# Block sums of the GRU gates over three PSUM tiles, and the last pair's update summed in the transposition

## Chip, cores and metric

One core of a Trainium2 chip. The metric is device time in microseconds, from the program's start to its end; lower is better.

## The reference

Sixty-four graphs of 256 nodes with 256 features. A layer norm with ReLU, then a message-passing layer with a convolution, ended by a GRU cell, and a residual:

```python
h = jnp.maximum(_layernorm(x, axis=-1), 0.0)
# of h: x_conv (two convolutions along the nodes, 1 and 17 taps, batch norms, ReLU, residual)
# of h: x_nmp = (exp(-dist) * adj) @ relu(h @ w_msg.T + b_msg)
x_in = jnp.concatenate([x_conv, x_nmp], axis=-1)
gi = x_in @ w_ih.T + b_ih
gh = h @ w_hh.T + b_hh
r = jax.nn.sigmoid(gi_r + gh_r)
z = jax.nn.sigmoid(gi_z + gh_z)
nn_ = jnp.tanh(gi_n + r * gh_n)
out = x + (1.0 - z) * nn_ + z * h
```

All of it is float32. The 17-tap convolution is done as products at chosen points (an FFT-like scheme in VectorE, products in TensorE), which the change does not touch.

## The kernel before, in words

**Batches, pairs, layout.** The loop `for b in range(NB)` (L1331) takes eight batches of eight graphs, each as four pairs of graphs. A pair's activations lie transposed: features on partitions in two halves (`dc` 0 and 1), and 512 columns, 256 for each of the two graphs (`g` 0 and 1). First comes the batch's convolution by products, then for each of the four pairs the gates (`gates`, L1188), with the next batch's first convolution, affinity and messages woven in.

**The gates.** A gate is a sum of products of weights with `h`, `xn` (x_nmp) and `xc` (x_conv). Both the weights and the activations are cut into two halves (features in and out, graphs), and a product of 2 x 2 blocks is made of seven block products instead of eight, with sums of blocks (`sums`, L1104, in VectorE) and sums of weights prepared ahead. `factors` (L1121) names the seven, and `part` (L1140) issues one of them: 6 matmuls of 256 columns for the r and z gates (`RZ`), 3 for the candidate (`NH`). In the trace each fp32 matmul stands as two instructions. `seven` (L1162) puts the seven together. It is called twice for each pair, first for r and z, then for the candidate.

**PSUM.** There are two rings: `aux`, four tiles of one bank (512 columns), and `acc`, two tiles of two banks (L580, L581). A ring hands its tiles out in the order in which the code asks. In `seven`, tile A = acc holds the sums of feature half 0 (one bank for each graph), E = acc those of half 1, and p5 = aux holds part 5 for a moment. The order recorded is:

- part 1 into A[:, 0]; ScalarE puts its negative into E[:, 0];
- part 5 into p5; ScalarE copies that to `e` in SBUF;
- part 2 onto A[:, 0]; part 6 onto E[:, 0];
- VectorE: A[:, 1] = E[:, 0] + e;
- part 7 onto E[:, 0]; VectorE: E[:, 1] = -E[:, 0] - e;
- part 3 onto A[:, 1]; half 0 is ready, `opened(0, A)`;
- part 4 onto E[:, 0]; half 1 is ready, `opened(1, E)`.

`opened` is `rz` (L1192; two tanh of 512 columns in ScalarE, to `tr` and to the slot of `tz`, shown as wb in the profile) or `n` (L1197; in ScalarE a bias pass and a copy of 512, then VectorE and a tanh for the candidate, the update h' = n + z (h - n), and copies to `back`, which a transposing transfer turns).

**The last pair** has no work after it that could cover its end. Its candidate pass is written out by hand (L1237 to L1253), in tiles of one bank, and ends in `last` (L1216), once for each feature half and graph: a bias pass in ScalarE, two steps in VectorE, tanh, a subtraction from h, a product with z, and two half-size steps that write `y_last`. `finish` (L1255) then transposes the eight 128 x 128 chunks of `y_last` in TensorE, adds x (`x_last`, shown as hh) and stores.

**What sets the order.** Every instruction goes through a `Recorder` (L250 on). It notes what each one reads and writes, and `plan` (L395) then issues all of them in an order of its own: it keeps a clock for each engine from estimated costs, gives every task a latest time counted back from TensorE's total, and takes for each engine the ready task with the earliest such time. So a small edit can change the order of instructions over the whole program. A PSUM tile counts as a whole in these dependences (`m = 1`, L280), both banks of an acc tile together. `nc.behind` adds a dependence by hand, and `nc.joined` keeps the four affinity products in one piece. Each engine then works in order. Since all go through the recorder, the profile puts nearly all of them at L378; instructions are told apart by their tiles. Slots of SBUF are shown as `wb`, whatever they hold.

Of the kernel before, what the change touches and what calls it, by code (L numbers as in the profile page):

```python
# [15 lines left out]
AF = mybir.ActivationFunctionType  # L16
ALU = mybir.AluOpType
# [477 lines left out]
def kernel(  # L495
# [18 lines left out]
    nc = Recorder(tc.nc)  # L514
    P = 128
    B, N, D = x.shape
    G = 2
# [4 lines left out]
    DC = D // P  # L522
    MC = N // P
    W = G * N
# [4 lines left out]
    L = 16  # L529
    NW = N // L  # L530
# [24 lines left out]
    Ut, Vt = (keep(n, SL) for n in ("U", "V"))  # L555
# [3 lines left out]
    ident = keep("ident", P)  # L559
    make_identity(tc.nc, ident)  # L560
    neg_half = keep("neg_half", G * MC)
# [18 lines left out]
    aux = Ring(psum.tile([P, W], FP, name=f"aux{k}") for k in range(4))  # L580
    acc = Ring(psum.tile([P, 2, W], FP, name=f"acc{k}") for k in range(2))  # L581
# [17 lines left out]
    def row_tile(t, g):  # L599
        return t[:, g * MC:(g + 1) * MC, :].rearrange("p c d -> p (c d)")  # L600
# [5 lines left out]
    def chunk(t, g, c):  # L606
        return t[:, g * N + c * P:g * N + (c + 1) * P]
# [3 lines left out]
    X, ADJ, HT, XNM, STATS = {}, {}, {}, {}, {}  # L611
# [117 lines left out]
    mm, transpose = nc.tensor.matmul, (lambda p, v: nc.tensor.transpose(p, v, ident))  # L729
    p = aux()  # L730
# [430 lines left out]

    def seven(i, unit, opened):  # L1162

        A = acc()
        part(A[:, 0], 1, i, unit, True)
        E = acc()
        nc.scalar.mul(E[:, 0], A[:, 0], -1.0)
        p5 = aux()
        part(p5, 5, i, unit, True)
        e = slots[ROLE["e"]].rearrange("p c d -> p (c d)")  # L1170
        nc.scalar.copy(e, p5)
        part(A[:, 0], 2, i, unit)
        part(E[:, 0], 6, i, unit)
        nc.vector.tensor_add(A[:, 1], E[:, 0], e)
        part(E[:, 0], 7, i, unit)
        nc.vector.scalar_tensor_tensor(E[:, 1], E[:, 0], -1.0, e, op0=ALU.mult, op1=ALU.subtract)
        part(A[:, 1], 3, i, unit)
        opened(0, A)
        part(E[:, 0], 4, i, unit)
        opened(1, E)  # L1180

    def halfs(p, k):
        return p[:, :, k * N:(k + 1) * N]

    def pieces(t):
        return t.rearrange("p (g n) -> p g n", n=N)

    def gates(i, between=None):  # L1188
        tr, gn = tr_tile, gn_tile
        tz = [slots[ROLE[f"tz{dc}"]].rearrange("p c d -> p (c d)") for dc in range(DC)]  # L1190

        def rz(dc, p):  # L1192
            for gate, t in ((0, tr[:, dc]), (1, tz[dc])):
                nc.scalar.activation(pieces(t), halfs(p, gate), AF.Tanh,
                                     bias=b_rz[:, gate * DC + dc:gate * DC + dc + 1], scale=0.5 - dc)

        def n(dc, p):  # L1197
            g = gn[:, dc]
            nc.scalar.activation(pieces(g), halfs(p, 1), AF.Identity,
                                 bias=b_hh[:, 2 * DC + dc:2 * DC + dc + 1], scale=1.0 - 2 * dc)  # L1200
            x = XNM[i][:, dc]
            nc.scalar.copy(pieces(x), halfs(p, 0))
# [12 lines left out]

        def last(dc, g, p):  # L1216
            a = slice(g * N, (g + 1) * N)
            v, d = gn[:, dc, a], tr[:, dc, a]
            nc.scalar.activation(v, p[:, N:], AF.Identity,
                                 bias=b_hh[:, 2 * DC + dc:2 * DC + dc + 1], scale=1.0 - 2 * dc)  # L1220
            nc.vector.scalar_tensor_tensor(v, d, 1.0, v, op0=ALU.add, op1=ALU.mult)
            nc.vector.scalar_tensor_tensor(v, v, 0.5, p[:, :N], op0=ALU.mult, op1=ALU.subtract if dc else ALU.add)
            nc.scalar.activation(v, v, AF.Tanh, bias=b_ih[:, 2 * DC + dc:2 * DC + dc + 1])
            nc.vector.tensor_sub(d, HT[i][:, dc, a], v)
            nc.vector.scalar_tensor_tensor(d, tz[dc][:, a], 1.0, d, op0=ALU.add, op1=ALU.mult)
            for c in range(MC):
                t = chunk(y_last[:, dc], g, c).rearrange("p (b h) -> p h b", b=NW)
                u, w = (q[:, c * P:(c + 1) * P].rearrange("p (h b) -> p h b", b=NW) for q in (d, v))
                nc.vector.scalar_tensor_tensor(t, u, 0.5, w, op0=ALU.mult, op1=ALU.add)

        seven(i, RZ, rz)
        if between:
            between()
        if i + 1 < NP:
            seven(i, NH, n)
            return
        a0, p5, e1, a1, e0 = aux(), aux(), aux(), acc()[:, 1], acc()[:, 0]  # L1237
        e = slots[ROLE["e"]].rearrange("p c d -> p (c d)")
        part(a0, 1, i, NH, True)
        nc.scalar.mul(e0, a0, -1.0)  # L1240
        part(p5, 5, i, NH, True)
        nc.scalar.copy(e, p5)
        part(a0, 2, i, NH)
        last(0, 0, a0)
        part(e0, 6, i, NH)
        nc.vector.tensor_add(a1, e0, e)
        part(e0, 7, i, NH)
        nc.vector.scalar_tensor_tensor(e1, e0, -1.0, e, op0=ALU.mult, op1=ALU.subtract)
        last(1, 1, e1)
        part(a1, 3, i, NH)  # L1250
        last(0, 1, a1)
        part(e0, 4, i, NH)
        last(1, 0, e0)  # L1253

    def finish(i):  # L1255
        if i + 1 < NP:
            t = gn_tile.rearrange("p c n -> p (c n)").bitcast(U16)
            nc.sync.dma_start_transpose(out=t.rearrange("p (k n) -> p k n", n=P), in_=back.bitcast(U16))
            if i % PB < PB - 1:
                deliver(i)  # L1260
            return
        for g in (1, 0):
            p, t = aux(), row_tile(x_last, g)
            for c in range(MC):
                for dc in range(DC):
                    transpose(p[:, c * D + dc * P:c * D + (dc + 1) * P], chunk(y_last[:, dc], g, c))
            nc.vector.tensor_add(t, p, t)
            nc.sync.dma_start(out=blocks(out, G * i + g), in_=t)

    def deliver(i):  # L1270
# [40 lines left out]
    b_rz = keep("b_rz", 2 * DC)  # L1311
# [19 lines left out]
    for b in range(NB):  # L1331
        i = b * PB
# [25 lines left out]
        if b == 0:  # L1358
            nc.emit()
            stage_ctx.close()  # L1360
            late = ctx.enter_context(tc.tile_pool(name="late", bufs=1, reuse_waits="tile"))
            w_x = late.tile([P, 3, len(IN), 3, P], FP, name="w_x")
            xnms = Ring(late.tile([P, DC, W], FP, name=f"xnm{k}") for k in range(2))
            gn_tile, tr_tile = (late.tile([P, DC, W], FP, name=n) for n in ("gn", "tr"))
            back = late.tile([P, DC * W], FP, name="back")
            hh, halves = (late.tile([P, 2 * MC, W], U16, name=n) for n in ("hh", "halves"))
            y_last = Ut[:, :DC * W].rearrange("p (c n) -> p c n", c=DC)
            x_last = hh.bitcast(FP).rearrange("p k d -> p (k d)").rearrange("p (q d) -> p q d", d=D)
        aggregate(i)
        begin(4)  # L1370
# [171 lines left out]
```

## Time and profile before

| | |
|---|---|
| median of 3 runs | 1669.55 us (1669.16 to 1672.69) |
| the profiled execution | 1671.88 us |
| its span, first to last instruction | 1670.1 us |
| TensorE busy, share of the span | 99%, 8984 matmul instructions |
| VectorE | 1456.8 us, 87% |
| ScalarE | 1127.2 us, 67% |
| GpSimd | 236.0 us, 14% |
| waits of TensorE for VectorE's acc | 7.8 us, 18 times |

How to read it: PE is TensorE, PEld its weight loads, DVE is VectorE, ACT is ScalarE, POOL is GpSimd, SP the queue of transfers. A group shows output <- inputs, with the tile's number left out. A number in brackets behind an instruction in the timeline is the idle time of its engine just ahead of it, and what ended it. Matmuls overlap, so the duration of a group of n is n steps and some 0.17 us of its last one's drain: 12 instructions of 256 columns last 2.75 us, and the next group starts 2.59 us after them.

### The profile page before, as it was taken

The numbers are of one execution on the slowest core, as the hardware profiler recorded it, in microseconds if no ns is written. First come the engines' busy times: TensorE is split into PE (matmuls) and PEld (weight loads), VectorE is DVE, ScalarE is ACT, GpSimd is POOL, SyncE is SP. The second block draws the span as 40 slices with busy tenths as digits, with TensorE's granted clock in tenths as the row PEclk, the third lists the DMA queues.
The fourth block names the chain that finished last, engine by engine and source line by source line (L and its number), as shares of the span: only waits on it lengthen the run. The fifth ranks groups of instructions, "written<-read, shape, count | busy, mean of one in ns | idle before, by whom it ended". The sixth has DMA issues, their size and how long they took to land.

```text
span 1670.1 us, 26281 instructions
## 1 busy us (share of the span) xinstructions
PE 1645.7 (99%) x8984; PEld 1413.3 (85%) x8984; DVE 1456.8 (87%) x3401; ACT 1127.2 (67%) x2029; POOL 236.0 (14%) x245
## 2 busy tenths in 40 slices
PE   9999999999999999999999999999999999999997
PEld 6888878978899788988889887897889978898886
DVE  7979989889889898898998988988988989789544
ACT  5546766776767767686756776677676776657554
POOL 4210210022110221103110131002211022000000
PEclk9999999999999999999999999999999999999999
DMA  9882557856468455783478654684647845375022
GB/s 250 301 291 75 135 109 203 264 110 147 108 202 227 105 123 126 237 205 95 114 139 265 151 122 103 176 259 110 146 108 207 222 108 133 83 231 142 16 61 51
DMA packets 314936, 261.37 MB, mean 156 GB/s; under 512 B 192875, under 2 KB 240263, under 8 KB 314802
## 3 DMA queue, kind: packets, MB, share of 16 engines
q1 hardware_dynamic: 297010, 216.71, 48.9%
q0 software_dynamic: 17376, 42.66, 11.3%
q8 instruction: 71, 1.16, 0.3%
q14 instruction: 63, 0.52, 0.1%
q10 hardware_dynamic: 416, 0.32, 0.1%
HBM read 156.60 MB, written 43.78 MB: 120 GB/s over the span
## 4 chain that ended last, share of the span: by engine, by line
PE 70%; DVE 24%; DMA 3%; issue 2%; ACT 1%; SPq 0%; DVEq 0%; ACTq 0%
PE acc L378 49%; PE aux L378 21%; DVE V L378 5%; DVE tr L378 3%; DVE U L378 3%; DVE T L378 3%; DVE wb L378 3%; DVE acc L378 2%; DVE gn L378 2%; DMA wb<-filt 2%; DVE st L378 1%; DVE PT L378 1%; DVE msg L378 1%; PE aux L374 1%; DVE Sv L378 0%
## 5 line engine op out<-in xcount | busy, mean ns | idle before, releaser
L378 PE MATMUL acc<-wb,w_ih 128*128 128x256 f32 x768 | 191.9, 379 | 0.0
L378 PEld LDWEIGHTS acc<-wb,w_ih 128*128 128x128 f32 x768 | 145.9, 190 | 19.8
L378 POOL DMA_DIRECT2D back<-in_x_dram x62 | 56.5, 1051 | 727.7 <-ACT back L378 379.5
L378 POOL TENSOR_TENSOR rstd<-rstd,neg_half 128x4 f32<-128x4 f32 x32 | 85.8, 2682 | 458.5 <-DVE shift L378 272.5
L378 PE MATMUL acc<-wb,w_x 128*128 128x256 f32 x576 | 136.9, 383 | 7.8 <-DVE acc L378 7.8
L378 ACT COPY back<-tr 128x512 uint16<-128x512 uint16 x124 | 128.3, 1078 | 22.5 <-DVE tr L378 22.2
L378 DVE SCALAR_TENSOR_TENSOR V<-T,V 128x128 f32<-128x128 f32 (+2 forms) x448 | 141.1, 379 | 0.0
L378 PE MATMUL aux<-wb,w_x 128*128 128x256 f32 x576 | 138.1, 382 | 0.0
L378 PEld LDWEIGHTS acc<-wb,w_x 128*128 128x128 f32 x576 | 106.9, 190 | 36.3 <-DVE acc L378 17.7
L378 PEld LDWEIGHTS aux<-wb,w_x 128*128 128x128 f32 x576 | 108.7, 191 | 17.3 <-DVE wb L378 2.6
L378 PE MATMUL aux<-w_msg,hT 128*128 128x259 f32 x512 | 121.7, 381 | 0.0
L378 PE MATMUL acc<-V,wb 128*128 128x128 f32 x1024 | 118.5, 275 | 0.8 <-DMA wb<-filt 0.8
L378 PEld LDWEIGHTS acc<-U,wb 128*128 128x128 f32 x1024 | 116.9, 192 | 2.6 <-ACT acc L378 1.7
L378 PE MATMUL acc<-U,wb 128*128 128x128 f32 x1024 | 117.2, 275 | 1.6 <-DMA wb<-filt 1.6
L378 PEld LDWEIGHTS acc<-V,wb 128*128 128x128 f32 x1024 | 116.4, 192 | 1.3 <-DMA wb<-filt 1.2
L378 ACT ACTIVATE gn<-acc,bn_columns 128x512 f32<-128x512 f32 (+1 forms) x64 | 43.5, 680 | 106.6 <-PE acc L378 101.5
L378 PE MATMUL acc<-Yv,w_ih 128*128 128x256 f32 x380 | 108.4, 381 | 2.1 <-ACT Yv L378 2.1
L378 PE MATMUL acc<-wb,w_hh 128*128 128x256 f32 x384 | 109.4, 380 | 0.7 <-ACT acc L378 0.7
L378 PEld LDWEIGHTS aux<-w_msg,hT 128*128 128x128 f32 x512 | 96.5, 190 | 14.3
L378 ACT COPY back<-gn 128x1024 uint16<-128x1024 uint16 x62 | 82.8, 1342 | 36.3 <-DMA gn<-back 36.3
L378 PE MATMUL aux<-hT,w_c 128*128 128x512 f32 x224 | 106.1, 592 | 0.0
L378 PE MATMUL acc<-hT,w_hh 128*128 128x256 f32 x380 | 104.0, 380 | 0.0
(200 smaller groups left out, 3898.3 us busy)
## 6 DMA issues: line engine op xcount, KB each, us to landing
wb<-filt SPq DMA_DIRECT2D x348, 256.0 KB
back<-in_x_dram POOLq DMA_DIRECT2D x62, 256.0 KB, 5.0
out_dram<-back POOLq DMA_DIRECT2D x62, 256.0 KB, 2.9
x<-in_x_dram SPq DMA_DIRECT2D x58, 256.0 KB
halves_d<-halves SPq DMA_DIRECT2D x28, 512.0 KB
adjh<-halves_d SPq DMA_DIRECT2D x112, 128.0 KB
hh<-halves SPq DMA_DIRECT2D x108, 128.0 KB
filt<-Yv POOLq DMA_DIRECT2D x18, 224.0 KB, 4.4
```

The lines of the kernel that those rows point to most:

```text
L374: self.tasks[k].call.append(lambda: method(*args, **kw))
L378: self.tasks.append(Task(engine, [lambda: method(*args, **kw)], cost, size, self.first))
```

## The change

It has two parts.

In `seven`, the sums are held in three tiles: a0 is the first bank of an acc tile (its second bank stays unused), a1 is the aux tile that held part 5 and is written over once part 5 has been copied, and E is an acc tile as before. Part 2 is recorded after part 6 and the add. As half 0 now lies in two tiles, `halfs` gives its eviction in two pieces of 256 columns.

For the last pair, the gate factors are brought into their final form before the candidate pass: tr becomes -r, a copy of tz becomes -z (in the free tile of the xnm ring), tz itself becomes z - 1, each in a ScalarE pass of 512 columns, and `z_last` = -z h is formed in VectorE. `last` then takes one VectorE step with the bias in it, one subtraction, the tanh, and one product with z - 1 into `y_last`; two of the four products are put behind the last subtraction. `finish` no longer transposes: products with the identity of `z_last` (behind the last gate matmul) and of `y_last` are summed in the same PSUM tile, and what comes out is subtracted from x.

```diff
     def seven(i, unit, opened):

-        A = acc()
-        part(A[:, 0], 1, i, unit, True)
+        a0 = acc()[:, 0]
+        part(a0, 1, i, unit, True)
         E = acc()
-        nc.scalar.mul(E[:, 0], A[:, 0], -1.0)
-        p5 = aux()
-        part(p5, 5, i, unit, True)
+        nc.scalar.mul(E[:, 0], a0, -1.0)
+        a1 = aux()
+        part(a1, 5, i, unit, True)
         e = slots[ROLE["e"]].rearrange("p c d -> p (c d)")
-        nc.scalar.copy(e, p5)
-        part(A[:, 0], 2, i, unit)
+        nc.scalar.copy(e, a1)
         part(E[:, 0], 6, i, unit)
-        nc.vector.tensor_add(A[:, 1], E[:, 0], e)
+        nc.vector.tensor_add(a1, E[:, 0], e)
+        part(a0, 2, i, unit)
         part(E[:, 0], 7, i, unit)
         nc.vector.scalar_tensor_tensor(E[:, 1], E[:, 0], -1.0, e, op0=ALU.mult, op1=ALU.subtract)
-        part(A[:, 1], 3, i, unit)
-        opened(0, A)
+        part(a1, 3, i, unit)
+        opened(0, (a0, a1))
         part(E[:, 0], 4, i, unit)
         opened(1, E)

-    def halfs(p, k):
-        return p[:, :, k * N:(k + 1) * N]
-
-    def pieces(t):
-        return t.rearrange("p (g n) -> p g n", n=N)
+    def halfs(t, p, k):
+        if isinstance(p, tuple):
+            return [(t[:, g * N:(g + 1) * N], p[g][:, k * N:(k + 1) * N]) for g in range(G)]
+        return [(t.rearrange("p (g n) -> p g n", n=N), p[:, :, k * N:(k + 1) * N])]
...
         def last(dc, g, p):
             a = slice(g * N, (g + 1) * N)
-            v, d = gn[:, dc, a], tr[:, dc, a]
-            nc.scalar.activation(v, p[:, N:], AF.Identity,
-                                 bias=b_hh[:, 2 * DC + dc:2 * DC + dc + 1], scale=1.0 - 2 * dc)
-            nc.vector.scalar_tensor_tensor(v, d, 1.0, v, op0=ALU.add, op1=ALU.mult)
-            nc.vector.scalar_tensor_tensor(v, v, 0.5, p[:, :N], op0=ALU.mult, op1=ALU.subtract if dc else ALU.add)
+            v = gn[:, dc, a]
+            nc.vector.scalar_tensor_tensor(v, p[:, N:], b_hh[:, 2 * DC + dc:2 * DC + dc + 1], tr[:, dc, a],
+                                           op0=ALU.subtract if dc else ALU.add, op1=ALU.mult)
+            nc.vector.tensor_sub(v, *((v, p[:, :N]) if dc else (p[:, :N], v)))
+            put = nc.last["vector"]
             nc.scalar.activation(v, v, AF.Tanh, bias=b_ih[:, 2 * DC + dc:2 * DC + dc + 1])
-            nc.vector.tensor_sub(d, HT[i][:, dc, a], v)
-            nc.vector.scalar_tensor_tensor(d, tz[dc][:, a], 1.0, d, op0=ALU.add, op1=ALU.mult)
-            for c in range(MC):
-                t = chunk(y_last[:, dc], g, c).rearrange("p (b h) -> p h b", b=NW)
-                u, w = (q[:, c * P:(c + 1) * P].rearrange("p (h b) -> p h b", b=NW) for q in (d, v))
-                nc.vector.scalar_tensor_tensor(t, u, 0.5, w, op0=ALU.mult, op1=ALU.add)
+            rest.append((y_last[:, dc, a], v, tz[dc][:, a]))
+            if (dc, g) == (1, 0):
+                for k, r in enumerate(rest):
+                    nc.behind = put if k in (1, 2) else None
+                    turned(*r)
+                nc.behind = None
+
+        def turned(o, u, v):
+            nc.vector.tensor_mul(o.rearrange("p (q b h) -> p q b h", h=L // 2, b=NW),
+                                 *(t.rearrange("p (q h b) -> p q b h", h=L // 2, b=NW) for t in (u, v)))
...
+        z = xnms.tiles[(xnms.n + 1) % 2]
+        for dc in range(DC):
+            for o, v, f in ((tr[:, dc], tr[:, dc], -0.5), (z[:, dc], tz[dc], -0.5), (tz[dc], tz[dc], 0.5)):
+                nc.scalar.activation(o, v, AF.Identity, bias=neg_half[:, :1], scale=f)
+            turned(z_last[:, dc], z[:, dc], HT[i][:, dc])
...
         part(p5, 5, i, NH, True)
         nc.scalar.copy(e, p5)
+        part(e0, 6, i, NH)
+        nc.vector.tensor_add(a1, e0, e)
         part(a0, 2, i, NH)
         last(0, 0, a0)
-        part(e0, 6, i, NH)
-        nc.vector.tensor_add(a1, e0, e)
         part(e0, 7, i, NH)
...
+        ps = [aux() for _ in range(G)]
+        for k, y in enumerate((z_last, y_last)):
+            nc.behind = None if k else nc.last["tensor"]
+            for g in (1, 0):
+                for c in range(MC):
+                    for dc in range(DC):
+                        o = c * D + dc * P
+                        mm(ps[g][:, o:o + P], chunk(y[:, dc], g, c), ident, start=k + o == 0, stop=k == 1,
+                           skip_group_check=True)
         for g in (1, 0):
-            p, t = aux(), row_tile(x_last, g)
-            for c in range(MC):
-                for dc in range(DC):
-                    transpose(p[:, c * D + dc * P:c * D + (dc + 1) * P], chunk(y_last[:, dc], g, c))
-            nc.vector.tensor_add(t, p, t)
+            p, t = ps[g], row_tile(x_last, g)
+            nc.vector.tensor_sub(t, t, p)
             nc.sync.dma_start(out=blocks(out, G * i + g), in_=t)
```

In `rz` and `n` (not shown) each eviction becomes a loop over the pieces that `halfs` returns.

More of the change, by code (lines that the diff above doesn't have):

```diff
@@ L1162, in seven @@
     def seven(i, unit, opened):
-        A = acc()
-        part(A[:, 0], 1, i, unit, True)
+        a0 = acc()[:, 0]
+        part(a0, 1, i, unit, True)
         E = acc()
-        nc.scalar.mul(E[:, 0], A[:, 0], -1.0)
-        p5 = aux()
-        part(p5, 5, i, unit, True)
+        nc.scalar.mul(E[:, 0], a0, -1.0)
+        a1 = aux()
+        part(a1, 5, i, unit, True)
         e = slots[ROLE["e"]].rearrange("p c d -> p (c d)")
-        nc.scalar.copy(e, p5)
-        part(A[:, 0], 2, i, unit)
+        nc.scalar.copy(e, a1)
         part(E[:, 0], 6, i, unit)
-        nc.vector.tensor_add(A[:, 1], E[:, 0], e)
+        nc.vector.tensor_add(a1, E[:, 0], e)
+        part(a0, 2, i, unit)
         part(E[:, 0], 7, i, unit)
         nc.vector.scalar_tensor_tensor(E[:, 1], E[:, 0], -1.0, e, op0=ALU.mult, op1=ALU.subtract)
-        part(A[:, 1], 3, i, unit)
-        opened(0, A)
+        part(a1, 3, i, unit)
+        opened(0, (a0, a1))
         part(E[:, 0], 4, i, unit)
         opened(1, E)
-    def halfs(p, k):
-        return p[:, :, k * N:(k + 1) * N]
-    def pieces(t):
-        return t.rearrange("p (g n) -> p g n", n=N)
+    def halfs(t, p, k):
+        if isinstance(p, tuple):
+            return [(t[:, g * N:(g + 1) * N], p[g][:, k * N:(k + 1) * N]) for g in range(G)]
+        return [(t.rearrange("p (g n) -> p g n", n=N), p[:, :, k * N:(k + 1) * N])]
     def gates(i, between=None):
-        tr, gn = tr_tile, gn_tile
+        tr, gn, rest = tr_tile, gn_tile, []
         tz = [slots[ROLE[f"tz{dc}"]].rearrange("p c d -> p (c d)") for dc in range(DC)]
@@ L1193, in rz @@
             for gate, t in ((0, tr[:, dc]), (1, tz[dc])):
-                nc.scalar.activation(pieces(t), halfs(p, gate), AF.Tanh,
-                                     bias=b_rz[:, gate * DC + dc:gate * DC + dc + 1], scale=0.5 - dc)
+                for o, v in halfs(t, p, gate):
+                    nc.scalar.activation(o, v, AF.Tanh, bias=b_rz[:, gate * DC + dc:gate * DC + dc + 1],
+                                         scale=0.5 - dc)
         def n(dc, p):
             g = gn[:, dc]
-            nc.scalar.activation(pieces(g), halfs(p, 1), AF.Identity,
-                                 bias=b_hh[:, 2 * DC + dc:2 * DC + dc + 1], scale=1.0 - 2 * dc)
+            for o, v in halfs(g, p, 1):
+                nc.scalar.activation(o, v, AF.Identity, bias=b_hh[:, 2 * DC + dc:2 * DC + dc + 1],
+                                     scale=1.0 - 2 * dc)
             x = XNM[i][:, dc]
-            nc.scalar.copy(pieces(x), halfs(p, 0))
+            for o, v in halfs(x, p, 0):
+                nc.scalar.copy(o, v)
             nc.vector.scalar_tensor_tensor(g, tr[:, dc], 1.0, g, op0=ALU.add, op1=ALU.mult)
@@ L1217, in last @@
             a = slice(g * N, (g + 1) * N)
-            v, d = gn[:, dc, a], tr[:, dc, a]
-            nc.scalar.activation(v, p[:, N:], AF.Identity,
-                                 bias=b_hh[:, 2 * DC + dc:2 * DC + dc + 1], scale=1.0 - 2 * dc)
-            nc.vector.scalar_tensor_tensor(v, d, 1.0, v, op0=ALU.add, op1=ALU.mult)
-            nc.vector.scalar_tensor_tensor(v, v, 0.5, p[:, :N], op0=ALU.mult, op1=ALU.subtract if dc else ALU.add)
-            nc.scalar.activation(v, v, AF.Tanh, bias=b_ih[:, 2 * DC + dc:2 * DC + dc + 1])
-            nc.vector.tensor_sub(d, HT[i][:, dc, a], v)
-            nc.vector.scalar_tensor_tensor(d, tz[dc][:, a], 1.0, d, op0=ALU.add, op1=ALU.mult)
-            for c in range(MC):
-                t = chunk(y_last[:, dc], g, c).rearrange("p (b h) -> p h b", b=NW)
-                u, w = (q[:, c * P:(c + 1) * P].rearrange("p (h b) -> p h b", b=NW) for q in (d, v))
-                nc.vector.scalar_tensor_tensor(t, u, 0.5, w, op0=ALU.mult, op1=ALU.add)
+            v = gn[:, dc, a]
[3 more added lines that the diff above has]
+            put = nc.last["vector"]
+            nc.scalar.activation(v, v, AF.Tanh, bias=b_ih[:, 2 * DC + dc:2 * DC + dc + 1])
+            rest.append((y_last[:, dc, a], v, tz[dc][:, a]))
[7 more added lines that the diff above has]
+                                 *(t.rearrange("p (q h b) -> p q b h", h=L // 2, b=NW) for t in (u, v)))
         seven(i, RZ, rz)
@@ L1367 @@
             y_last = Ut[:, :DC * W].rearrange("p (c n) -> p c n", c=DC)
+            z_last = Ut[:, DC * W:2 * DC * W].rearrange("p (c n) -> p c n", c=DC)
             x_last = hh.bitcast(FP).rearrange("p k d -> p (k d)").rearrange("p (q d) -> p q d", d=D)
```

## The prediction

> **What bounds the kernel now.** I read the page first, then TensorE's waits, then its timeline in a middle batch, and last the timeline and the chain of the end. On the page (engine, busy us, share of the span, instructions), and in the seven 198 us stretches that follow each other from 230 us on (one batch each; of which one row):
>
> ```profile
> PE 1645.7 (99%) x8984; PEld 1413.3 (85%) x8984; DVE 1456.8 (87%) x3401; ACT 1127.2 (67%) x2029; POOL 236.0 (14%) x245
> ...
> 626.00:824.00 198.00, 197.03 (x1082) 169.88 (x1081) 179.78 (x421) 139.88 (x249) 28.17 (x24) 1.00 0.62 158
> ```
>
> TensorE is the bound, and nearly full: a batch has under 1 us in which it does nothing. A change can gain only in TensorE's own work, in its few waits, and at the end. These are its waits (who waited for whom: us in all, times, longest):
>
> ```profile
> PE acc L378 <- DVE acc L378: 7.8, 18, 0.7
> PE aux L378 <- DVE U L378: 3.6, 2, 3.4
> PE acc L378 <- DMA wb<-filt: 2.4, 2, 1.6
> PE acc L378 <- ACT Yv L378: 2.1, 1, 2.1
> PE aux L378 <- POOL e L378: 1.8, 1, 1.8
> ...
> PE acc L378 <- ACT acc L378: 0.7, 1, 0.7
> ```
>
> The first row is the change's main target. A middle batch shows what it is:
>
> ```profile
> 426.42 1.89 PE L378 MATMUL acc<-wb,w_ih 128*128 128x256 f32 x8
> 428.24 0.71 PE L374 MATMUL aux<-zT 9*128 9x256 f32 x8
> 429.39 2.86 PE L378 MATMUL acc<-wb,w_x 128*128 128x256 f32 x12 [0.45 <-DVE acc L378]
> ...
> 445.88 1.46 PE L378 MATMUL aux<-e,msg 128*128 128x256 f32 x6
> 447.18 1.46 PE L378 MATMUL acc<-wb,w_x 128*128 128x256 f32 x6
> ```
>
> At 426.42 part 6 of the r and z gates runs. VectorE's add of E[:, 0] and e into A[:, 1] follows it, and part 7 (acc<-wb,w_x) may not overwrite E before that add has read it. Part 2 is spent already, so the planner has only the four affinity products as cover, and TensorE stands 0.45 us. At 445.88, in the candidate gate, six instructions of 1.30 us stand in the same place and there is no wait: that much cover suffices. The wait comes twice in each of the six middle batches and three times in the first and in the last, 18 in all. And the end:
>
> ```profile
> 1653.55 0.70 PE L378 MATMUL acc<-wb,w_hh 128*128 128x256 f32 x2 [0.67 <-ACT acc L378]
> ...
> 1659.26 1.03 PE L378 MATMUL acc<-wb,w_ih 128*128 128x256 f32 x4
> ...
> 1663.81 0.33 PE L378 MATMUL aux<-ident,U 128*128 128x128 f32 x1 [3.37 <-DVE U L378]
> ...
> 1665.34 1.35 DVE L378 TENSOR_TENSOR hh<-aux,hh 128x512 f32<-128x512 f32 x2
> ```
>
> The last gate matmul ends at about 1660.1. Then VectorE and ScalarE work alone (the chain has the stretch from 1660.5 to 1664.3 in VectorE's gn, tr and U, with 0.2 us of issue); eight transposes, two adds of x and the store follow. From the last add's end, 1666.69, to the span's end are 3.4 us of store.
>
> [...] the 0.45 us come back at 627.5, 825.4 and 1023.3. [...] The kernel's recorder is coarser: it treats an acc tile of two banks as one, so the add into A[:, 1] also waits for part 2 in A[:, 0]; that is why part 2 stands before part 6 and is no cover. [...] Here the stretch 1538.0 to 1541.7, after a wait of 2.1 us, has a granted clock of 0.57. [...] The trace has one instruction for a transpose and two for an fp32 product with 128 columns, 0.114 us apart (acc<-U,wb, 64 in 7.32 us at 1510.5).
>
> **The change part by part.**
>
> *Three tiles.* The second sum moves from A's second bank to the aux tile that held part 5. The add no longer touches part 2's tile, so part 2 goes behind part 6. In the changed program's order this holds for every r/z and candidate pass: parts 1, 5, 6, 2, 7, 3, 4, and the affinity products come after the r/z pass. Part 2 has 12 instructions x 0.216 = 2.59 us in r/z and 6 x 0.216 = 1.30 us in the candidate; the add needs some 0.2 us from TensorE's end, 0.70 us for itself and 0.05 us to release, 0.95 us. Both cover it. Gain: 7.8 us, bounds 5 (a third comes back, as VectorE can be in another instruction of up to 1.2 us when part 6 ends) and 7.8.
>
> *Part 6 now comes directly after part 5.* It needs -A in E. In the candidate E becomes free only when the r/z pass's second eviction is done: 0.2 + 2 x 0.59 (tr, wb) + 0.59 (the negation) + 0.05 = 2.0 us after part 4, against parts 1 and 5, 2 x 1.30 = 2.6 us. Hidden, with 0.6 us to spare. Where exps or `back` copies stand between on ScalarE the order has other work between too: affinity 0.9 us, in some pairs conv1, 1.7 us. Cost 0; without that cover 0.3 us in each of 16 passes, 4.8 us.
>
> *ScalarE.* The first sum's eviction is cut in halves: 64 more instructions in r/z, 62 in the candidate. Two of 256 columns cost 0.38 us each, start to start (the two gn tanhs of 256 columns before 1661.6), against 0.59 for one of 512: 0.17 us x 126 = 21 us at most, against 543 us in which ScalarE idles. Who waits: acc's first bank is evicted before part 3 even runs, so the next pass is freed earlier; the aux half has part 4's 2.59 us as cover against 0.2 + 2 x 0.38. Cost 0.
>
> *aux held longer.* a1 keeps one of four aux tiles from part 5 to its eviction, some 14 us rather than 3.5. Affinity and message take all four and so come after part 3. The order shows other parts in their old places. No row prices what is late then: between 0 and 3 us, I take 1.0. SP's transfers and POOL's change place by a few positions; TensorE waits for a transfer only twice, 2.4 us, before the first gate: 0.
>
> *The end.* Per `last` three VectorE instructions and one ScalarE go in place of six and two. Six ScalarE passes of 512 (0.59) and two products of 512 columns (the permuted e<-e,adj of 256 takes 0.51 from start to start, so 1.0 each) come ahead, under parts 1 to 6. On ScalarE only one of them stands before the negation that releases part 6: 0.2 + 3 x 0.59 + 0.59 = 2.6 us against 2.6 of parts 1 and 5. So the 0.67 us wait goes, and part 4 ends some 0.7 to 0.9 us earlier, at about 1659.3. From there: 0.2, the first VectorE step 0.35, the subtraction 0.41, under the two products that are put behind it 0.9 (the tanh, 0.55, hides there), the last product 0.5: 1661.7. TensorE meanwhile does z times h: 8 x 2 x 0.114 = 1.8 us. The y products follow, 1.8 us, half of them before the last factor is there: to about 1662.9; the last subtraction from x, 0.2 + 0.7: 1663.9, where it was 1666.69. Gain 2.8 us with the 0.67 in it; bounds 1.3 (the permuted products take 0.8 each) and 3.6.
>
> Sum: -7.8 - 2.8 + 1.0 = -9.6 us. The profiled execution took 1671.88 us (span 1670.1 and 1.8 around it): 1662.3. The median shown is 1669.55, 2.3 lower; I set the forecast against it: 1660.0.
>
> **The rivals.**
>
> *B, half comes back as waits for ScalarE.* Part 6 lost part 2 as its cover. At 16 passes x 0.3 us = 4.8 us the time is 1669.55 - 9.6 + 4.8 = 1664.8. For it: ScalarE's queue is in order and has 1.3 us copies in it. Against it: only one wait of TensorE for ScalarE's acc is in the trace, 0.7 us.
>
> *C, the waits only move.* Part 2 is no new work; what it covers it leaves uncovered elsewhere. Then the end alone gains: 1669.55 - 2.8 = 1666.8, inside 0.2%. Against it: at 445.88 other work is the cover today; part 2 takes its place, and that work is set free rather than missing.
>
> *D, slower.* ScalarE's `back` copies wait in line for the transposing transfers (36.3 us in 15 waits, the longest 4.8). In the changed order they stand directly behind the evictions of a1 and ahead of the exps and of E's eviction. If that transfer lands late, parts 1 to 5 no longer cover it: 15 waits x (2.4 - 0.9) = 22 us, less 10.6: 1681. It decides from a landing more than 0.9 us after a1's eviction. The trace has these copies start at 832.4 with no wait, in the same phase, which speaks against it.
>
> **How the numbers follow.** A (as summed, 1657.5 to 1662.5) 0.70; better than that, to 1656.5 with the larger end (3.6) and without the half-clock window at 1538 [...] 0.04; B 0.14; C 0.07; D 0.05. The range 1656.5 to 1665 holds A, the better case and most of B. About 0.2%, 3.3 us, is what a measurement can tell here from no change. Faster: A, the better case and B, 0.88; same: C, 0.07; slower: D, 0.05.
>
> **What would show it.** Right: TensorE's row of waits for VectorE's acc falls from 7.8 to under 2 us; part 2 stands between parts 6 and 7 with no idle time; no wait of TensorE for ScalarE's acc over 1 us in all; the batches are 0.9 to 1.0 us shorter; the idle 3.4 us at the end are filled by 16 products; the last add to x ends 2 to 3.5 us sooner after the last r/z pass. Wrong: new rows of TensorE waiting for ScalarE's acc or tr (B, D), or for aux tiles (the 1.0), or batches still 198 us long (C).

## The result, and the profile after

After: 1671.49 us (median; 1667.87 to 1676.59). Before, on the same chip: 1670.06 us. The ratio is 1.0009, 95% interval 1.0002 to 1.0016: no gain, if anything 0.1% longer, where 1660.0 was forecast. The profiled execution took 1671.57 us, its span 1669.8.

Of the page after, the same row as before (engine, busy us, share, instructions), and then TensorE's waits (us in all, times, longest):

```profile
PE 1652.6 (99%) x9008; PEld 1417.0 (85%) x9008; DVE 1459.3 (87%) x3391; ACT 1148.6 (69%) x2157; POOL 242.5 (15%) x245
```

```profile
PE acc L378 <- DVE acc L378: 2.8, 3, 1.9
PE aux L378 <- DVE wb L378: 2.6, 6, 0.5
PE acc L378 <- ACT acc L378: 2.4, 1, 2.4
PE acc L378 <- ACT Yv L378: 2.1, 1, 2.1
PE aux L378 <- POOL e L378: 1.8, 1, 1.8
PE acc L378 <- DVE hT L378: 0.6, 1, 0.6
PE acc L378 <- DMA wb<-filt: 0.3, 1, 0.3
```

The 18 waits of 7.8 us are gone. Three others for VectorE's acc have come (1.90, 0.65 and 0.20 us, all ahead of part 4, which needs the second sum), six for wb, and one of 2.4 us for ScalarE's acc. In the timeline of TensorE, the affinity products (zT) no longer end in a wait, but one batch is as long as it was, 1034.67 to 1232.56 = 197.89 us (before: 1023.31 to 1221.20, 197.89 too):

```profile
1034.03 0.71 PE L374 MATMUL aux<-zT 9*128 9x256 f32 x8
1034.67 0.70 PE L378 MATMUL acc<-wb,w_ih 128*128 128x256 f32 x2
...
1231.91 0.71 PE L374 MATMUL aux<-zT 9*128 9x256 f32 x8
1232.56 0.70 PE L378 MATMUL acc<-wb,w_ih 128*128 128x256 f32 x2
```

The end did what was forecast. The gate's last product is followed at once by the sums with the identity, and the adds to x come sooner:

```profile
1660.96 1.03 PE L378 MATMUL acc<-wb,w_ih 128*128 128x256 f32 x4
1661.82 3.83 PE L378 MATMUL aux<-ident,U 128*128 128x128 f32 x32
...
1665.02 1.36 DVE L378 TENSOR_TENSOR hh<-hh,aux 128x512 f32<-128x512 f32 x2 [0.52 <-PE aux L378]
```

From the first product of the last r/z pass to the end of the span, before took 38.1 us and after 35.3. So this stretch became 2.8 us shorter (how much of it is the end's own is seen below), and the last pair began 2.5 us later than before, where up to 6.8 us earlier was forecast.

**Where it was lost.** Two stretches of the timeline of after show it. First VectorE and TensorE near the end of a batch:

```profile
806.40 0.75 DVE L378 SCALAR_TENSOR_TENSOR T<-U 128x256 f32<-128x256 f32 x2
809.83 0.43 DVE L378 BATCH_NORM_STATS2 st<-x 128x6 f32<-128x256 f32 x1 [2.68 <-DMA x<-in_x_dram]
...
811.57 0.69 DVE L378 SCALAR_TENSOR_TENSOR acc<-acc,wb 128x512 f32<-128x512 f32 x1
...
812.32 0.70 PE L378 MATMUL acc<-wb,w_hh 128*128 128x256 f32 x2 [1.90 <-DVE acc L378]
812.86 1.52 PE L378 MATMUL acc<-wb,w_ih 128*128 128x256 f32 x4
814.18 3.12 PE L378 MATMUL aux<-hT,w_c 128*128 128x512 f32 x4
```

The statistics of the next x wait 2.68 us for their transfer. Behind them and three more instructions stands the gate's second sum, acc<-acc,wb, which part 4 needs: TensorE waits 1.90 us. Then it runs at half clock (granted clock 0.50 from 813.24 to 816.65): four products of 512 columns take 3.12 us, elsewhere 1.88. The same place costs 0.65 us of wait in the next batch and 0.20 in an earlier one. Second, ScalarE, VectorE and TensorE ahead of the first gates of a batch:

```profile
1129.79 1.36 ACT L378 COPY hT<-hh 128x1024 uint16<-128x1024 uint16 x1 [0.53 <-DMA hh<-halves]
...
1131.49 1.20 ACT L378 ACTIVATE e<-aux 128x256 f32<-128x256 f32 x4
...
1131.89 2.12 DVE L378 TENSOR_TENSOR e<-e,adj 128x256 f32<-128x256 f32 x4 [0.50 <-ACT e L378]
...
1148.10 0.68 DVE L378 TENSOR_TENSOR wb<-Yv 128x512 f32<-128x512 f32 x1
...
1148.84 1.13 PE L378 MATMUL aux<-wb,w_x 128*128 128x256 f32 x4 [0.52 <-DVE wb L378]
```

A copy into hT waits 0.53 us for its transfer and then takes 1.36 us, ahead of the exps. VectorE, which has no other idle time until 1148.8, waits 0.50 us for the first exp, and is that much late with the sum of xc, for which part 5 waits. Neither wait is on a transfer by its name; both begin at one. The rows of VectorE and ScalarE that wait for these two transfers, before:

```profile
ACT hT L378 <- DMA hh<-halves: 1.6, 2, 1.4
...
DVE st L378 <- DMA x<-in_x_dram: 4.6, 3, 3.9
```

and after:

```profile
ACT hT L378 <- DMA hh<-halves: 4.8, 6, 1.7
...
DVE st L378 <- DMA x<-in_x_dram: 12.3, 9, 3.9
```

### The profile page after: what moved, and what is told of

Same layout as the page of the kernel before. It is cut to its first block, busy times and chain, and to the rows that moved or that the text cites. A ratio compares the mean times of both kernels' runs of the same rounds, so it can differ in the third digit from the quotient of the medians.

```text
span 1669.8 us, 26552 instructions
## 1 busy us (share of the span) xinstructions
PE 1652.6 (99%) x9008; PEld 1417.0 (85%) x9008; DVE 1459.3 (87%) x3391; ACT 1148.6 (69%) x2157; POOL 242.5 (15%) x245
## 4 chain that ended last, share of the span: by engine, by line
PE 79%; DVE 12%; DMA 4%; issue 2%; ACT 1%; SPq 1%; POOL 1%; ACTq 0%; DVEq 0%
PE acc L378 50%; PE aux L378 28%; DVE V L378 3%; DVE T L378 2%; DMA hh<-halves 2%; DVE Yv L378 2%; DVE wb L378 1%; DMA x<-in_x_dram 1%; PE aux L374 1%; DVE e L378 1%; SPq L378 1%; DMA wb<-filt 1%; POOL shift L378 1%; DVE msg L378 1%; DVE st L378 0%
## 5 line engine op out<-in xcount | busy, mean ns | idle before, releaser
L378 POOL TENSOR_TENSOR rstd<-rstd,neg_half 128x4 f32<-128x4 f32 x32 | 79.3, 2478 | 432.4 <-DVE shift L378 275.5
L378 PE MATMUL acc<-wb,w_hh 128*128 128x256 f32 x384 | 105.7, 384 | 5.1 <-DVE acc L378 2.8
L378 DVE TENSOR_TENSOR e<-e,adj 128x256 f32<-128x256 f32 x128 | 68.7, 596 | 46.7 <-ACT e L378 46.7
L378 PE MATMUL acc<-Yv,w_ih 128*128 128x256 f32 x380 | 103.2, 381 | 2.1 <-ACT Yv L378 2.1
L378 PE MATMUL acc<-xnm,w_ih 128*128 128x256 f32 x380 | 104.0, 380 | 0.0
```

The costliest lines, as they stand in the source:

```text
L378: self.tasks.append(Task(engine, [lambda: method(*args, **kw)], cost, size, self.first))
```

## The experiments

**Theory O**: the waits did go, but the planner wrote another order of work, and in it instructions that wait for a transfer stand in the in-order queues of VectorE and ScalarE ahead of gate steps. **Rivals**: S, the split evictions and the aux tile held longer cost it; P, a batch cannot be shorter than 197.9 us; E, the two parts of the change disturb each other; L, the order itself is worse, whatever waits for transfers. Each ratio is to before, measured on the same chip. The runs come from several chips, on which before's median lay between 1670.06 and 1671.07 us, so where two runs are compared with each other, the ratios are the better measure.

**One part alone.** First the new `seven`, `halfs`, `rz` and `n` with the old end; then the old ones with the new end.

> The three PSUM tiles alone; the last pair and the end stay as they were before. Theory O (the eighteen waits went, but the order of work that the planner then writes puts instructions that wait for transfers, and VectorE's sums, ahead of gate steps that TensorE needs): the end gains nothing here, so this is the changed kernel plus 2.7 us, about 1674 us, ratio to before 1.002 to 1.003, with the new waits of TensorE for VectorE's wb (six of about 0.4 us) in its trace. Theory E (the changed end is what disturbs the rest, and the tiles gain their 7.8 us): 1662 us, ratio 0.995.

Measured: 1677.24 us, ratio 1.0041 (1.0028 to 1.0053).

> The changed last pair and end alone; the gates of all other passes stay as they were before, two sums in one tile of two banks. Its order of work is the same as before's up to the last pair. Theory O: only the end changes, 2.7 us less, 1667.3 us, ratio 0.9984. Theory E: the six ScalarE passes and the products brought forward cost something in the last pair and the gain is under 1 us, ratio 0.9995 or more.

Measured: 1669.03 us, ratio 0.9993 (0.9985 to 1.0001). So the loss lies in the tiles and E falls, but both sizes miss: by the ratios the end gives 1.2 us here, and 5.3 us on top of the tiles (1.0041 to 1.0009).

The traces say where. From the first product of the last r/z pass to the end of the span, before took 38.1 us, the tiles alone 37.3, the end alone 36.6 and both 35.3. So with the tiles in place the end is worth 2.0 us, and the tiles 0.9 us in the last r/z pass. With the end alone, part 6 of the last pair waits 1.2 us for ScalarE's acc (before 0.67). The rest between the tiles alone and both lies ahead of the last pair, although by the traces each engine has the same instructions there in the same order. The tiles alone, for one, have a wait of TensorE of 2.16 us for VectorE's aux at 194.79, which the profiled run of both has not. So the waits of one and the same order differ in length from execution to execution.

**Only the order.** The next kernel has the instructions of the changed one. One line of the planner differs, in which it reckons when a transfer has landed:

```diff
-                t.done = self.dma + 1.1
+                t.done = self.dma + 3.1
```

> The changed kernel, but the planner is told that every transfer lands 2 us later; no instruction is added or removed, only the order of work moves. Theory O: instructions that wait for a transfer go further back in VectorE's and ScalarE's queues, the waits behind the x loads (2.68, 1.42 and 0.99 us) go, and the time falls by 2 to 6 us, to 1666 to 1669.5 us, ratio to before 0.9975 to 0.9998. Theory S (the cost lies in the split evictions and the aux tile that is held longer, whatever the order): 1671 to 1672 us, ratio 1.001.

Measured: 1666.06 us, ratio 0.9971 (0.9962 to 0.9981). 5.4 us from order alone, as O has it, and S falls. But its middle batches are still 197.9 us long. The gain lies in the first batch and in the two batches in which the changed kernel waited 1.90 and 0.65 us for VectorE's acc (3.1 and 1.0 us shorter). That left P open.

The statistics of x were also put behind the gate's second sum by hand, by taking them out of `between` and recording them in `seven`:

```diff
         nc.vector.scalar_tensor_tensor(E[:, 1], E[:, 0], -1.0, e, op0=ALU.mult, op1=ALU.subtract)
+        if after is not None:
+            stats(after, nc.last["vector"])
         part(a1, 3, i, unit)
```

> The changed kernel, but in the three middle gates of a batch VectorE's statistics of the next x are put behind the second sum of the candidate pass (they still compute the same). Theory O: the wait of 1.90 us of TensorE for VectorE's acc and the half-clock window that follows it (1.7 us more) go, and the shorter ones with them: 2 to 5 us less than the changed kernel, 1666.5 to 1669.5 us, ratio to before 0.998 to 0.9997. Theory S: no change against the changed kernel, ratio 1.001.

Measured: 1688.19 us, ratio 1.0114 (1.0099 to 1.013). A miss, on the other side. No wait for VectorE's acc is left; in its place, of TensorE's waits:

```profile
PE acc L378 <- ACT acc L378: 7.8, 5, 1.9
PE aux L378 <- DVE wb L378: 5.8, 7, 1.0
PE acc L378 <- ACT V L378: 3.8, 5, 1.5
PE aux L378 <- ACT hT L378: 3.0, 3, 1.8
```

Later statistics make the normalization, the transposing transfer and the copies into hT later: ScalarE's waits of hT for hh rise from 4.8 us in 6 waits to 16.5 us in 22. Moving one culprit back makes its successors late. The planner wrote a new order here too.

**The same line with other values, with and without the tiles.**

> The changed kernel, with the planner told that every transfer lands 1 us later (the earlier run had 2 us). Theory O: what came back lies in the order of work alone, so an order that keeps the sum for xc ahead of part 5 and the x statistics behind the second gate sum has both: batches 0.7 to 1.0 us shorter than 197.9 us and no wait behind an x load, 1660 to 1664 us, ratio to before 0.994 to 0.9965. Theory P (a batch cannot be shorter than 197.9 us, since something other than TensorE's waits sets its pace; only the waits for transfers can be won): batches of 197.9 us again and 1665.5 to 1667.5 us.

Measured (`self.dma + 2.1`): 1657.68 us, ratio 0.9924 (0.9911 to 0.9936), better than both kernels and than Theory O's range. Its span is 1655.2 us; of the timeline of TensorE and of the waits:

```profile
1023.78 0.70 PE L378 MATMUL acc<-wb,w_ih 128*128 128x256 f32 x2
...
1220.62 0.70 PE L378 MATMUL acc<-wb,w_ih 128*128 128x256 f32 x2
```

```profile
PE acc L378 <- ACT Yv L378: 2.1, 1, 2.1
PE aux L378 <- POOL e L378: 1.8, 1, 1.8
PE aux L378 <- DVE wb L378: 1.5, 2, 1.1
```

A batch is 196.84 us, 1.05 less, and TensorE waits for neither VectorE's nor ScalarE's acc. P falls, and S once more: evictions and tiles are those of the changed kernel. VectorE and ScalarE wait for the two transfers thus (hT has no row at all):

```profile
DVE st L378 <- DMA x<-in_x_dram: 4.1, 2, 3.8
```

Its partners have the old gates and the new end:

> The gates as before, the changed end, and the planner told that every transfer lands 1 us later: the partner of the run with the three tiles and the same estimate. Theory O: the waits behind the affinity products stay, so it lies 3 to 7 us over that partner, 1666.5 to 1670 us. Theory T (the tiles bring nothing, the landing estimate brings the whole gain): the same as the partner within 1.5 us.

Measured: 1673.68 us, ratio 1.002 (1.0012 to 1.0028).

> The gates as before, the changed end, and the planner told that every transfer lands 2 us later: the partner of the run that gave 1666.06 us with three tiles. Theory O: 1667 to 1673 us, the order being another draw with the old waits in it. Theory T (the landing estimate brings the whole gain): 1665 to 1667 us.

Measured: 1677.52 us, ratio 1.0043 (1.0031 to 1.0055). So the estimate brings nothing by itself. What the tiles do at equal estimate, by the ratios: +2.7 us with the estimate as it is (1.0009 against 0.9993), -16.0 with 1 us more (0.9924 against 1.002), -12.0 with 2 us more (0.9971 against 1.0043). Each is one order against another, and orders of the same instructions lie between 1657.68 and 1688.19 us.

> The changed kernel, with the planner told that every transfer lands 0.5 us later (the run with 1 us gave 1657.68 us, the changed kernel with 0 gave 1671.49 us). Theory O: another draw of the order; the gate's waits are gone, and what it costs is what stands behind a transfer in line: 1658 to 1668 us. Theory M (the estimate is simply too low, and the time falls steadily as it rises to the right value): about halfway, 1664 to 1665 us.

Measured: 1668.16 us, ratio 0.9979 (0.9969 to 0.9988), at the upper edge of O's range. The time doesn't fall steadily with the estimate (0, 0.5, 1, 2 us: 1671.5, 1668.2, 1657.7, 1666.1), so M falls: each value is another draw of the order.

The margin for one engine only, where `lag` gave 0 for every transfer (the second kernel has 1.0 and "scalar"):

```diff
-        return 0.0 if u.size else (self.OWN if u.engine == v.engine else self.LAG)[u.engine]
+        if u.size:
+            return 2.0 if v.engine == "vector" else 0.0
+        return (self.OWN if u.engine == v.engine else self.LAG)[u.engine]
```

> The changed kernel, with the planner told only that VectorE sees a transfer 2 us after its landing; ScalarE and the queues are planned as in the changed kernel. Theory O: VectorE's wait for an x load ahead of the second gate sum goes, and with it the waits of TensorE for VectorE's acc (2.8 us) and the half-clock window behind the longest (1.7 us): 1664 to 1668 us, ratio to before 0.996 to 0.9985; the batches without such a wait stay at 197.5 to 197.9 us. Theory S (the split evictions and the aux tile held longer are the cost): 1670.5 to 1672 us.

Measured: 1664.52 us, ratio 0.9967 (0.9953 to 0.998), as O has it, though the batches are shorter than it said (197.1 us).

> The changed kernel, with the planner told only that ScalarE sees a transfer 1 us after its landing; VectorE is planned as in the changed kernel. Theory O: ScalarE's copies that wait for a transfer go behind the exps and the negation, so that the six waits of TensorE for VectorE's wb (2.6 us) and the one for ScalarE's acc in the first batch (2.4 us and its half-clock window) go; the batches are 0.7 to 1.0 us shorter; waits for x loads may stay: 1657 to 1663 us, ratio 0.992 to 0.9955. Theory V (VectorE's waits for x loads are the cause, ScalarE's are covered): 1669 to 1671 us.

Measured: 1659.35 us, ratio 0.9931 (0.9918 to 0.9943), as O has it; V falls. Both are new orders too, so they don't yet tell O from L.

**The order kept, the transfer taken out of it.** In each of these three kernels the planner works with the true inputs, and only then is the call replaced, so that the order is that of the kernel it came from (in the traces every engine has the same instructions in the same order, but for the inputs replaced):

```diff
-            nc.vector.bn_stats(s[:, j, :], X[i][:, j, :])
+            k = nc.vector.bn_stats(s[:, j, :], X[i][:, j, :])
+            if i > PB:
+                nc.tasks[k].call = [lambda j=j: nc.nc.vector.bn_stats(s[:, j, :], w_c1[:, j % DC, :])]
```

> The changed kernel in its own order of work, instruction for instruction, but from the sixth pair on VectorE's statistics read a weight tile that is always there in place of x, so that they wait for no transfer (the statistics and what is normalized with them are not the reference's; every transfer still runs). Theory O: the waits of TensorE for VectorE's acc (2.8 us), the half-clock window behind the longest (1.7 us) and the stall of 0.2 us ahead of part 4 in each batch (1.3 us) go: 5 to 6 us less than 1671.49, 1665.5 to 1667 us, ratio to before 0.997 to 0.998. Theory L (the order itself is worse, whatever waits in it for transfers): 1670.5 to 1672 us.

Measured: 1667.22 us, ratio 0.998 (0.9971 to 0.9988): 4.3 us less than the changed kernel (4.8 by the ratios), a little under the 5 to 6. Of TensorE's waits, none is for VectorE's acc.

```diff
-            nc.scalar.copy(v[:, j], u[:, j])
+            k = nc.scalar.copy(v[:, j], u[:, j])
+            w = HT[i - 1].bitcast(U16).rearrange("p c (n j) -> p j c n", j=2)
+            nc.tasks[k].call = [lambda j=j, w=w: nc.nc.scalar.copy(v[:, j], w[:, j])]
```

> As the run before, and ScalarE's copies into hT read the hT of the pair before in place of hh, so that they wait for no transfer either (hT from the sixth pair on is not the reference's; order and transfers are untouched). Theory O: the wait of 0.53 us of ScalarE in each batch no longer delays the exps, so VectorE's sum for xc comes earlier and the six waits ahead of part 5 (2.6 us, 3.2 with the stall behind each) go, and part of the 2.4 us in the first batch: 3 to 6 us less than the run before, 1660 to 1664 us, ratio 0.994 to 0.9965; the batches are 196.8 to 197.1 us. Theory L: within 1 us of the run before.

Measured: 1662.21 us, ratio 0.9952 (0.9939 to 0.9966): 5.0 us less again. The batches are 197.2 us, just above what was expected, since the sum of xc is still late by 0.3 us in this order:

```profile
PE acc L378 <- ACT acc L378: 3.1, 1, 3.1
PE acc L378 <- ACT Yv L378: 2.1, 1, 2.1
PE aux L378 <- POOL e L378: 1.8, 1, 1.8
PE aux L378 <- DVE wb L378: 1.7, 6, 0.3
```

> The same two substitutions in the kernel before, in its own order. Theory O: before has no such wait on its path, so it stays within 1 us of 1670.5 us, ratio 0.9994 to 1.0005, its batches 197.9 us and its eighteen waits of 7.8 us all there. Theory L, or a gain that comes from the substitutions as such: as much less as in the changed kernel, 1660 to 1665 us.

Measured: 1670.5 us, ratio 1.0 (0.9992 to 1.0008), with 8.0 us in 17 waits for VectorE's acc. The same substitutions bring nothing before and 9.3 us after (9.5 by the ratios). So for these 9 us L falls: it is the waits for the two transfers.

**The end once more**, with the tiles and the estimate of the best run:

> The three tiles alone, the last pair and the end as before, with the planner told that every transfer lands 1 us later: the run of 1657.68 us without the changed end, in the same order up to the last pair. Theory O: the end brings its 2.8 us here as in the other order, 1660.5 us, ratio to before 0.994. Theory E (the end's gain depends on the order, as 1.4 us in one pair of runs and 5.7 us in another suggest): under 1.5 us or over 4.5 us.

Measured: 1661.56 us, ratio 0.9941 (0.9929 to 0.9954), as O has it. The medians differ by 3.9 us, but they come from two chips; by the ratios (0.9941 and 0.9924) it is 2.8 us, with intervals too wide to tell these apart. The traces do better: from the first product of the last r/z pass to the end of the span it is 37.3 us here and 35.3 in the best run, 2.0 us as in the other order. What else differs in the profiled runs lies ahead of that, in part in the granted clock, whose mean over the span is 0.997 here and 1.000 in the best run.

**The price of a wait.** In the best run's order VectorE's second sum was repeated, more often from batch to batch:

```diff
         nc.vector.scalar_tensor_tensor(E[:, 1], E[:, 0], -1.0, e, op0=ALU.mult, op1=ALU.subtract)
+        if unit is NH and i % PB == 1 and 0 < i // PB < NB - 1:
+            nc.tasks[nc.last["vector"]].call *= 1 + i // PB
```

> The run with landings 1 us later (1657.68 us), its order of work untouched, but VectorE's second sum of the candidate gate is done 2, 3, 4, 5, 6 and 7 times over instead of once, in one candidate pass of each of the six middle batches (the repeats write the same values). It makes waits of TensorE of growing length at one known place, about 0.6 us more from batch to batch less 0.4 us of slack: 0.2, 0.8, 1.4, 2.0, 2.6 and 3.2 us, 10 us in all. Theory H (a wait of about 2 us is followed by 3.4 us of half clock, which costs 1.7 us more): the last three are, 5 us in all, 1673 us, ratio to before 1.0015. Theory W (a wait costs itself alone): 1668 us, ratio 0.9985.

Measured: 1675.21 us, ratio 1.0032 (1.002 to 1.0045), 17.5 us more than without the repeats. TensorE's waits in the timeline:

```profile
611.28 0.70 PE L378 MATMUL acc<-wb,w_hh 128*128 128x256 f32 x2 [0.72 <-DVE acc L378]
809.84 0.70 PE L378 MATMUL acc<-wb,w_hh 128*128 128x256 f32 x2 [1.45 <-DVE acc L378]
1009.13 0.70 PE L378 MATMUL acc<-wb,w_hh 128*128 128x256 f32 x2 [2.19 <-DVE acc L378]
1209.15 1.22 PE L378 MATMUL acc<-wb,w_hh 128*128 128x256 f32 x2 [2.92 <-DVE acc L378]
1412.37 0.70 PE L378 MATMUL acc<-wb,w_hh 128*128 128x256 f32 x2 [3.61 <-DVE acc L378]
```

The four batches with waits of 0.72, 1.45, 2.19 and 3.61 us became longer by 0.97, 1.71, 2.44 and 3.86: here a wait costs itself and 0.25 us. Only the one of 2.92 us was followed by half clock (granted clock 0.50 from 1209.15 to 1212.56); its batch, in which ScalarE's acc is also waited for (0.64 us), became 5.68 longer. The other 2.8 us of the 17.5 lie outside these five batches, some 1.6 of them at half clock by an estimate from the mean granted clock (0.998 over 1673.4 us, a loss of 3.3 us, 1.7 of it behind the wait of 2.92 us; the run without the repeats has 1.000). Theory H is half right: half clock followed the wait of 2.92 us, but the longer one of 3.61 us was followed by a granted clock of 1.00, so length alone doesn't decide (see the last section).

## Why the prediction was wrong, step by step

- **Three tiles, gain 7.8 us**: the mechanism was right, part 2 covers the add in every pass. In the best run's order a batch is 1.05 us shorter for two waits, a little more than the 0.9 of their idle time: with the wait, the next product started 1.17 us after the affinity's first (1022.14 to 1023.31 in before), and without it 0.64 us after (1034.03 to 1034.67 in after). In the changed kernel as much came back in the same batch: 0.52 us of wait ahead of part 5, and about 0.2 us each there and at two other places where a product stood just short of its operand.
- **Part 6 directly after part 5, cost 0** and **the split evictions, cost 0**: right in the best run, where TensorE waits for no acc of VectorE or ScalarE. ScalarE's busy time rose by 21.4 us in the changed kernel (21 reckoned at most). There part 6 waits once, 2.4 us in the first batch.
- **aux held longer, 1.0 us**: not seen: neither the changed kernel nor the best run has a row of TensorE waiting for a free aux tile that before has not.
- **The step that failed**: "SP's transfers and POOL's change place by a few positions; TensorE waits for a transfer only twice, 2.4 us, before the first gate: 0". TensorE was the wrong place to look. VectorE and ScalarE wait for transfers, in order, with gate steps behind them (2.68 us for x and 0.53 us for hh in the stretches above). The planner reckons 1.6 us, the size (1.59 here) and 1.1 us from an x load's issue to its landing, 4.3 us. In the trace of after one was issued at 802.51, and the statistics could start at 809.83, 7.3 us later. Before, such waits were fewer (4.6 us in 3 for x, against 12.3 us in 9), and the substitutions show that from the sixth pair on none of them held TensorE up. After, these two kinds of wait cost some 9 of the 11.5 us by which the forecast missed (9.3 by the medians).
- **The rest, some 2 us**, is of the size of what is left in the first batch: there a `back` copy waits 1.60 us and a copy into hT 1.74 us for their transfers, the negation for part 6 comes behind them, and TensorE waits 2.4 us with half clock following (granted clock 0.50 from 209.08 to 212.49). In the run with both substitutions this wait is still there, 3.1 us, and the best run, which has not got it, is 4.5 us shorter. It was not tried alone, so this part is argued and not shown.
- **The end, 2.8 us**: the mechanism was right, and the gain inside its bounds of 1.3 to 3.6, but the end's own part is 2.0 us. That before and after differ by just 2.8 us from the last r/z pass on is luck: 0.9 of it is the tiles' part in that pass.
- **The rivals**: C gave the likeness (batches of 197.9 us, the end alone gains; 0.07). D named the mechanism (ScalarE's copies wait in line for transfers, 0.05), but priced it at the `back` copies in every pass. It came from hT and, in VectorE, from x, in few places. B came in one place, the 2.4 us ahead of part 6 in the first batch, and not in 16 passes.

## What to carry to other kernels

Where a planner orders the whole program, a local edit is priced in two parts: what it takes away in place, and what the new order puts in front of the critical steps. Look in the new order for every instruction that waits for a transfer and has a step of the critical path behind it in its queue, on the engines that feed the busy one, and compare the planner's assumed landing with the trace. And before a change is given up, let the planner draw again with several margins, and measure each: here the best of four values of one constant turned 1671.5 into 1657.7 us, while another gave 1668.2, and with the old gates both values tried made the time longer.

## What the hardware showed unexpectedly

**Half clock followed some waits and not others.** Half clock is a stretch in which the granted clock is 0.50. In the trace of after the stretches of half clock begin at 209.08, 813.24 and 1543.69 us, and each lasts 3.41. Of the last two, the granted clock (PEclk) and TensorE's busy time (PE, after the length) in the 3.41 us ahead and in the stretch itself:

```profile
809.83:813.24 3.41, 1.51 (x6) 0.84 (x5) 3.41 (x8) 1.29 (x3) 0.00 (x0) 1.00 1.08 187
813.24:816.65 3.41, 3.41 (x6) 1.68 (x6) 3.41 (x9) 1.79 (x3) 0.00 (x0) 0.50 0.55 122
1540.28:1543.69 3.41, 1.70 (x7) 1.19 (x8) 3.41 (x8) 3.21 (x10) 0.59 (x2) 1.00 0.85 180
1543.69:1547.10 3.41, 3.41 (x10) 2.70 (x9) 3.41 (x7) 0.89 (x2) 0.55 (x1) 0.50 0.24 84
```

TensorE was without work for 1.90 and 1.71 us of the time ahead. In the run with the repeats half clock followed the wait of 2.92 us (first row), and none followed the wait of 3.61 us (second row, third row behind it):

```profile
1209.15:1212.56 3.41, 3.41 (x7) 2.53 (x8) 3.08 (x7) 0.44 (x1) 0.00 (x0) 0.50 0.30 61
1408.76:1412.37 3.61, 0.00 (x1) 0.00 (x1) 3.47 (x6) 0.78 (x1) 0.00 (x0) 1.00 0.23 46
1412.37:1415.78 3.41, 3.41 (x13) 2.25 (x14) 3.41 (x8) 1.46 (x3) 0.00 (x0) 1.00 0.62 138
```

The wait of 2.19 us there was followed by 1.00 too (1009.13 to 1012.54). So whether a wait of 2 to 3.6 us cost 1.7 us more, half of the 3.41, was not a matter of its length alone. What else decides was not shown. That half clock is one source of the spread between executions is an estimate from those 1.7 us and two traces: in the profiled run of before TensorE's wait of 2.09 us for ScalarE's Yv ended at 1538.03 and half clock followed (0.50 from 1538.50 to 1541.91); in that of the end alone, which has the same order there, this wait was 2.1 us and the mean granted clock of the span 1.000.
